# dt and B with all 128 rows in layer 1, and the side work's balance by place

## The chip, the cores and the metric

The kernel runs on one core of one Trainium2 chip. A core has five engines that work side by side and wait for one another through semaphores: TensorE (PE: multiplies and transposes, from SBUF into PSUM), VectorE (DVE), ScalarE (ACT), GpSimd (POOL) and SyncE (SP, which here issues transfers). PEld is TensorE's loading of weights. The metric is the device time of one execution in microseconds, and the number told is the median of several runs.

## The reference

Two layers work on an image of 256 x 256 positions with 128 channels, in fp32; each adds its result to the image. Layer 0 is triangle attention over rows. Layer 1, which the change touches, is a window scan:

```python
x = x + _L0_conv_ref(_gn(x), ...)          # triangle attention
x = x + _L1_conv_ref(_gn(x), ...)          # window scan
# in _L1_conv_ref
x_dbl = jnp.einsum('bkdl,kcd->bkcl', xs, x_proj_w)
dts, Bs, Cs = jnp.split(x_dbl, [DT_RANK, DT_RANK + D_STATE], axis=2)
dts = jnp.einsum('bkrl,kdr->bkdl', dts, dt_projs_w)
dts = jax.nn.softplus(dts + dt_projs_b[None, :, :, None])
def step(h, inp):
    u, dt, Bl, Cl = inp
    dA = jnp.exp(dt[..., None] * A)
    h = h * dA + (dt * u)[..., None] * Bl[:, :, None, :]
    y = jnp.einsum('bkdn,bkn->bkd', h, Cl)
    return (h, y)
```

Each image position is expanded to 256 inner channels, convolved 3 x 3 per channel, gated with silu, and cut into windows of 8 x 8. Two windows are merged into a sequence of 128 steps, which is walked in four ways (K = 4): two orders, each forward and backward. dt has rank 8 (DT_RANK), the state has 16 entries (D_STATE). After the scan come a layer norm, a gate from z, and a projection back to 128 channels.

## The kernel before, in words

**Bands, jobs, units.** Layer 1 is cut into 64 bands of 16 image rows by 64 columns. A band has two groups of four sequences, and each group is walked in two orders (`o`): so there are four jobs a band and 256 in all. A job is 32 units: two directions (`back`), four quarters of the state (`q`), two halves of the inner channels (`dh`), two halves of the sequences (`p`). A unit's number modulo 32 is its place in the job.

**A unit's work.** `decay` (L1172, ScalarE) makes exp(dt*A), four instructions for two units. `input` (L1185, TensorE) makes dt*u*B in PSUM, in the tile `b_p`, which has two buffers: it multiplies rows of `dut` (the transposed dt*u) with a diagonal arrangement of B, 64 rows at a time. `scan` (L1205, VectorE) runs the recurrence over 1024 columns. `weigh` (L1212, GpSimd) multiplies two units' states with C. `reduce` (L1223, TensorE) adds the weighed states into `y_p` by transposes, 16 for two units.

**The order.** The loop from L1333 writes each engine's order out by hand. At an even unit i it issues the decay of units i+4 and i+5, the input of unit i+1, the scan of unit i and the input of unit i+2. At an odd unit it issues the scan, the weigh of the pair, and the reduce of the pair two behind. `input` of unit i+2 needs the buffer that the scan of unit i frees.

**A job's preparation.** `own_script` (L1118) prepares the next job at fixed places: u at 7 and 9, `xd` (dt's 8 raw rows for each direction with a row of ones for the bias, then B, then C, 128 rows in all) at 15 to 17, B's transposes `bt_mm` at 18, their copy `bt_ev` at 19, and the forward dt at 20 to 26; `script` (L1091) does the backward dt at 0 to 6. Each dt is made in two halves: a matmul `dt_mm` into PSUM, softplus's Exp and Ln on ScalarE a unit later (`dt_act`), then one operation on VectorE (`dt_max`, L1034) at the places 2, 6, 22 and 26. `xd`, `bt`, `dt` and others share one PSUM buffer, named `side`. The copy `bt` is sent to DRAM by eight small transfers (`spread`, place 20), into zeroed blocks from which B's diagonal arrangement is read back. `xd`'s last 32 rows go to DRAM as C.

**The balance of side work.** What belongs to no job (the in projection, the convolution, the gate, the norm, the out projection) is a queue of small steps, `Filler`, each with a cost: columns of TensorE where positive, 0 for ScalarE's steps, -2 for VectorE's, which run at even units alone. At each unit the credit rises by `rate` columns up to `cap`; the job's own calls at this place are taken off it; and at odd units steps of TensorE are run while the credit is no less than their cost less `slack`. After a step of another engine, no step of TensorE follows in that unit.

Of the kernel before, what the change touches and what calls it, by code (L numbers as in the profile page):

```python
# [12 lines left out]
F32 = mybir.dt.float32  # L13
# [6 lines left out]
P = 128  # L20
# [5 lines left out]
DI = 256  # L26
NS = 16
DTR = 8
# [8 lines left out]
NBLK = 4  # L37
# [30 lines left out]
def kernel(  # L68
# [28 lines left out]
    nc = tc.nc  # L97
# [10 lines left out]
    ident = const.tile([P, P], F32, name="ident")  # L108
# [50 lines left out]
    wts = ctx.enter_context(tc.tile_pool(name="wts", bufs=1))  # L159
# [8 lines left out]
    for dh in range(2):  # L168
        nc.scalar.dma_start(
            out=wtap[:, dh], in_=conv_w[:, dh * P : (dh + 1) * P].rearrange("t d -> d t")  # L170
# [5 lines left out]
    for dh in range(2):  # L176
        for k in range(KD):
            o, back = k % 2, k // 2
            for at, lo, n in (
# [5 lines left out]
                    out=wx[:, dh, o, at : at + n],  # L185
                    in_=x_proj[dh * P : (dh + 1) * P, k, lo : lo + n],
                )

    wdt = wts.tile([P, 2, DI], F32, name="wdt")
    for back in range(2):  # L190
        at = 32 * back
        nc.scalar.dma_start(
            out=wdt[at : at + DTR], in_=dt_w[:, 2 * back : 2 * back + 2]
        )
        for o in range(2):
            for dh in range(2):
                j = 2 * (o + 2 * back) + dh
                nc.scalar.dma_start(
                    out=wdt[at + DTR : at + DTR + 1, o, dh * P : (dh + 1) * P],
                    in_=dt_b[:, j : j + 1].rearrange("p j -> j p"),  # L200
                )
    units_at = wts.tile([P, 1], F32, name="units_at")
# [13 lines left out]


    perm = wts.tile([P, 2, P], F32, name="perm")
    permt = wts.tile([P, 2, P], F32, name="permt")
    halves_of = ident.rearrange("p (y f x) -> p y f x", y=WIN, f=2)  # L220
    for o, positions in enumerate(hilbert_positions()):
        for s, (wy, wx_) in enumerate(positions):
# [1 line left out]
                perm[:, o, 2 * s : 2 * s + 2], halves_of[:, wy, :, wx_]  # L224
            )
    with tc.tile_pool(name="pmp", bufs=1, space=PSUM) as pp:
        pt_p = pp.tile([P, 2, P], F32, name="pt_p")
        for o in range(2):
            nc.tensor.transpose(pt_p[:, o], perm[:, o], ident)
        nc.vector.tensor_copy(permt, pt_p)  # L230

        ca_p = pp.tile([P, P], F32, name="ca_p")
        nc.tensor.matmul(ca_p, perm[:, 0], perm[:, 1], start=True, stop=True)
        carry = wts.tile([P, P], F32, name="carry")
        nc.vector.tensor_copy(carry, ca_p)
# [25 lines left out]
    with tc.tile_pool(name="lnc", bufs=1) as cp, tc.tile_pool(  # L261
        name="lnx", bufs=3
    ) as xp, tc.tile_pool(name="lnt", bufs=3) as tp, tc.tile_pool(
        name="lnp", bufs=2, space=PSUM
# [9 lines left out]
        for k in range(KD):  # L274
            for nh in range(2):
                for blk in range(NBLK):
                    nc.scalar.dma_start(
                        out=bdiag[k][nh][blk].rearrange("p t n -> p (t n)"), in_=zero
# [33 lines left out]
    with tc.tile_pool(name="atc", bufs=1) as cp, tc.tile_pool(  # L312
        name="atx", bufs=7
    ) as xp, tc.tile_pool(name="att", bufs=3) as tp, tc.tile_pool(
        name="ats", bufs=8
    ) as wp, tc.tile_pool(name="atps", bufs=1, space=PSUM) as ps_s, tc.tile_pool(
        name="atpt", bufs=1, space=PSUM
    ) as ps_t, tc.tile_pool(name="atpm", bufs=1, space=PSUM) as ps_m, tc.tile_pool(
        name="atpo", bufs=1, space=PSUM
# [11 lines left out]
        for mc in range(2):  # L331
            nc.sync.dma_start(
                out=trib[:, :, mc, :],
                in_=tri_d[:, mc * P : (mc + 1) * P, :].rearrange("h p n -> p h n"),
# [333 lines left out]
    class Band:  # L668
# [125 lines left out]
        def finish(self, g):  # L794

            if self.gated is None:
                self.gated = one_p.tile([P, 2, NSEQ, SEQ], F32, name="gated")
            for s2 in range(GS // 2):
                s = g * GS + 2 * s2
                yield 512  # L800
                z_p = fill("z_p")
                for dh in range(2):
                    nc.tensor.matmul(
                        z_p[:, dh * DI : (dh + 1) * DI],
                        win[:, DI + dh * P : DI + (dh + 1) * P],
                        self.xg[:, 1 : 1 + WIN, :, 1 + s * WIN : 1 + (s + 2) * WIN]
                        .rearrange("p y f x -> p (y f) x")
                        .rearrange("p y (s x) -> p s y x", s=2),
                        start=True,
                        stop=True,  # L810
                    )
                yield -2

                ysum = self.ysb[g, 1][:, 2 * s2 : 2 * s2 + 2]
                e = two_p.tile([P, 512], F32, name="e")
                nc.vector.tensor_scalar(e, z_p, FLOOR, None, ALU.max)
                st = two_p.tile([P, 2, 6], F32, name="st")
                mv = two_p.tile([P, 2, 2], F32, name="mv")
                for j in range(2):
                    nc.vector.bn_stats(st[:, j], ysum[:, j])  # L820
                for j in range(2):
                    nc.vector.bn_aggr(mv[:, j], st[:, j])
                yield 0
                logistic(e)
                rs = two_p.tile([P, 2], F32, name="rs")
                rsqrt(rs, mv[:, :, 1])
                neg = two_p.tile([P, 2], F32, name="neg")
                nc.scalar.activation(neg, rs, AF.Copy, scale=-1.0)
                nb = two_p.tile([P, 2], F32, name="nb")
                for j in range(2):  # L830
                    nc.scalar.activation(
                        nb[:, j : j + 1],
                        mv[:, j, 0:1],
                        AF.Identity,
                        scale=neg[:, j : j + 1],
                    )
                yield -2
                nc.vector.tensor_mul(e, e, z_p)
                yn = one_p.tile([P, 2, DI], F32, name="yn")
                for j in range(2):  # L840
                    nc.scalar.activation(
                        yn[:, j],
                        ysum[:, j],
                        AF.Identity,
                        bias=nb[:, j : j + 1],
                        scale=rs[:, j : j + 1],
                    )
                yield 256
                w_p = fill("w_p")
                for dh in range(2):  # L850
                    for j in range(2):
                        nc.tensor.transpose(
                            w_p[:, dh * DI + j * P : dh * DI + (j + 1) * P],
                            yn[:, j, dh * P : (dh + 1) * P],
                            permt[:, 1],
                        )
                yield 0
                for dh in range(2):
                    half = w_p[:, dh * DI : (dh + 1) * DI]
                    nc.scalar.activation(  # L860
                        half,
                        half,
                        AF.Identity,
                        bias=lb1[:, dh : dh + 1],
                        scale=lw1[:, dh : dh + 1],
                    )
                yield -2
                nc.vector.tensor_mul(
                    self.gated[:, :, s : s + 2].rearrange("p d s l -> p d (s l)"),
                    w_p.rearrange("p (d l) -> p d l", d=2),  # L870
                    e.rearrange("p (d l) -> p d l", d=2),
                )
# [26 lines left out]
    def token_blocks(t):  # L899

        return t.rearrange("c (h s t) -> c h s t", h=2, s=GS)
# [5 lines left out]
    class Job:  # L907
# [53 lines left out]
        def bt_mm(self):  # L961
            self.c_d = cdr.tile([2 * NS, GT], F32, name="c_d")
            for h in range(2):
                nc.sync.dma_start(
                    out=token_order(self.c_d)[:, h],
                    in_=token_blocks(self.xd[96:128])[:, h],
                )
            self.bt_p = side("bt_p")
            for i in range(NBLK):
                nc.tensor.transpose(  # L970
                    self.bt_p[:, i * 32 : (i + 1) * 32],
                    self.xd[64:96, i * P : (i + 1) * P],
                    ident[64:96, 64:96],
                )

        def bt_ev(self):
            self.bt = two_p.tile([P, NBLK, 2, NS], F32, name="bt")
            nc.scalar.copy(
                self.bt.rearrange("p b k n -> p (b k n)"), self.bt_p[:, 0 : NBLK * 32]
            )  # L980

        def spread(self):
# [31 lines left out]

        def dt_mm(self, back, dh):
            self.dt_p = side("dt_p")
            rows = slice(32 * back, 32 * back + DTR + 1)
            nc.tensor.matmul(  # L1018
                token_order(self.dt_p),
                wdt[rows, self.o, dh * P : (dh + 1) * P],  # L1020
                token_blocks(self.xd[rows]),
                start=True,
                stop=True,
            )
# [93 lines left out]
        def own_script(self):  # L1118
# [6 lines left out]
                15: [(512, lambda: self.xd_mm(0))],  # L1125
                16: [(512, lambda: self.xd_mm(1))],
                17: [(0, lambda: self.xd_ev())],
                18: [(128, lambda: self.bt_mm())],
                19: [(0, lambda: self.bt_ev())],
                20: [(512, lambda: self.dt_mm(0, 0)), (0, lambda: self.spread())],  # L1130
                21: [(0, lambda: self.dt_act(0, 0))],
# [159 lines left out]

    rate, cap, slack = 350, 800, 128
    with tc.manual_schedule():
        bands[0].load()
        run(bands[0].normalise(), bands[0].expand(), bands[0].conv(0))
# [5 lines left out]
        for c in range(2):  # L1303
            job, back, q = quads[c]
# [28 lines left out]
        for i, unit in enumerate(units):  # L1333
# [15 lines left out]
            if i % 2:  # L1349
# [4 lines left out]
                if i >= 5:  # L1354
                    units[i - 5].reduce()
                    units[i - 4].reduce()
            credit = min(credit + rate, cap)
            for cost, call in calls:
                credit -= cost
                call()  # L1360
# [81 lines left out]
```

## Time and profile before

| What | Value |
|---|---|
| Median of 3 runs | 23599.31 us (23597.42 to 23599.98) |
| Profiled execution | 23598.3 us, its span 23596.4 us |
| Granted TensorE clock, mean | 0.997 |
| PE busy | 22824.2 us, 97% |
| DVE busy | 21652.4 us, 92% |
| ACT busy | 18542.0 us, 79% |
| POOL busy | 21292.1 us, 90% |

The profile is of one execution. A row of a group shows the line and engine, the operation and its tiles (written <- read), its shape and count, then its busy time and mean length in ns, and after the bar how long the engine idled just before it and for whom. A row of the timeline shows start and length in us; neighbours of the same line are merged. The ends of TensorE's instructions are modelled, their starts are recorded.

### The profile page before, as it was taken

To read this page: it belongs to the slowest core of one execution; us is meant where nothing else is said; L and a number is where in the kernel's file an instruction comes from. 1 tells how busy PE (TensorE), PEld (TensorE's weight loads), DVE (VectorE), ACT (ScalarE), POOL (GpSimd) and SP (SyncE) were. 2 spreads that over 40 slices of the span, in tenths; PEclk is the share of its full clock that TensorE was granted. 3 is DMA by queue.
4 is the path that set the end of the run, shared out by engine and by line. 5 is a ranking of instruction groups with operands and counts; after the bars stand their busy time and mean duration, and the time that the engine had idled before them with its cause. 6 is when DMAs were issued, how large, how long until landed. Compare 5 with 4: busy or idle time off the path is not lost.

```text
span 23596.4 us, 427303 instructions
## 1 busy us (share of the span) xinstructions
PE 22824.2 (97%) x171020; PEld 16986.3 (72%) x171020; DVE 21652.4 (92%) x17940; ACT 18542.0 (79%) x35206; POOL 21292.1 (90%) x5966
## 2 busy tenths in 40 slices
PE   7999999999999999999999999999999999999999
PEld 2555677777777777777777777777777777777777
DVE  6888899999999999999999999999999999999998
ACT  5999777777777777777777777777777777777777
POOL 3777899999999999999999999999999999999999
PEclk9999999999999999999999999999999999999999
DMA  5222444444444444444444444444444444444444
GB/s 200 76 74 72 146 160 159 161 162 160 161 158 162 161 160 159 160 163 160 161 159 160 162 160 162 158 161 162 160 159 161 162 161 160 158 161 162 160 160 147
DMA packets 2000327, 3638.76 MB, mean 154 GB/s; under 512 B 1129584, under 2 KB 1131760, under 8 KB 1725824
## 3 DMA queue, kind: packets, MB, share of 16 engines
q1 hardware_dynamic: 1985616, 3602.35, 45.7%
q8 instruction: 1347, 22.07, 0.4%
q10 hardware_dynamic: 12720, 9.07, 0.1%
q14 instruction: 644, 5.28, 0.1%
HBM read 3467.33 MB, written 143.65 MB: 153 GB/s over the span
## 4 chain that ended last, share of the span: by engine, by line
PE 67%; DVE 16%; ACT 9%; issue 8%; DMA 0%; ACTq 0%; POOLq 0%; SPq 0%; POOL 0%; DVEq 0%
PE b_p L1185 23%; PE y_p L1223 21%; DVE h L1205 14%; PE dt_p L1018 4%; PE cv_p L769 4%; PE xd_p L949 2%; ACT da L1172 2%; PE aT_p L522 1%; PE dut_p L1052 1%; PE sc L465 1%; ACT w_p L860 1%; PE in_p L721 1%; PE o_p L885 1%; ACT e L132 1%; PE v_p L383 1%
## 5 line engine op out<-in xcount | busy, mean ns | idle before, releaser
L1212 POOL TENSOR_TENSOR h<-h,cc 128x2048 f32<-128x2048 f32 x4096 | 18598.0, 4551 | 1318.2 <-POOL h L1212 560.7
L1205 DVE TENSOR_TENSOR_SCAN h<-da,b_p 128x1024 f32<-128x1024 f32 x8192 | 18245.8, 2271 | 1212.6 <-PE b_p L1185 1193.2
L1172 ACT ACTIVATE da<-dt,am 128x508 f32<-128x508 f32 x16384 | 10396.5, 707 | 853.3 <-DVE h L1205 853.2
L1185 PE MATMUL b_p<-diag,dut 64*128 64x256 f32 x65536 | 8561.4, 395 | 430.0 <-DVE h L1205 365.7
L1223 PEld LDWEIGHTS y_p<-ident,h 128*128 128x128 f32 x65536 | 7130.2, 140 | 1408.4 <-issue 1296.3
L1223 PE MATMUL y_p<-ident,h 128*128 128x128 f32 x65536 | 8008.8, 276 | 25.1 <-issue 19.4
L1185 PEld LDWEIGHTS b_p<-diag,dut 64*128 64x128 f32 x65536 | 5851.7, 186 | 2916.9 <-issue 1331.2
L738 ACT ACTIVATE tap<-xin,wtap 128x512 f32<-128x512 f32 x2048 | 1504.2, 744 | 349.1 <-PE cv_p L769 349.0
L1041 POOL TENSOR_TENSOR du<-dt,u 128x512 f32<-128x512 f32 x1024 | 1309.1, 1278 | 57.9 <-DVE dt L1034 57.9
L769 PE MATMUL cv_p<-ident,tap 128*128 128x128 f32 x9216 | 1273.7, 275 | 5.1 <-DVE xct L788 3.8
L769 PEld LDWEIGHTS cv_p<-ident,tap 128*128 128x128 f32 x9216 | 1047.4, 141 | 232.4 <-issue 228.2
L1028 ACT ACTIVATE sp<-dt_p 128x512 f32<-128x512 f32 x1024 | 603.1, 589 | 777.5 <-PE dt_p L1018 777.5
L452 POOL TENSOR_TENSOR tm<-trib,mb 128x2048 f32<-128x2048 f32 x256 | 1167.1, 4559 | 10.7
L1018 PE MATMUL dt_p<-xd,wdt 9*128 9x512 f32 x2048 | 1149.8, 641 | 2.5 <-DVE dt L1034 2.2
L493 ACT ACTIVATE at<-at,nmax 128x256 f32<-128x256 f32 x2048 | 1019.5, 502 | 0.0
L1061 ACT COPY dut<-dut_p 128x512 f32<-128x512 f32 x1024 | 583.8, 570 | 292.9 <-PE dut_p L1052 292.9
L1163 ACT ACTIVATE da<-ident 128x16 f32<-128x16 f32 x1536 | 346.0, 225 | 549.2 <-DVE h L1205 547.4
L1029 ACT ACTIVATE sp<-sp,one 128x512 f32<-128x512 f32 x1024 | 743.1, 726 | 33.3
L729 ACT COPY xin<-in_p 128x440 f32<-128x440 f32 x384 | 201.7, 525 | 718.6 <-PE in_p L721 718.6
L478 DVE CUSTOM_DVE_ANT_0 at<-sc,tm 128x256 f32<-128x256 f32 x2048 | 738.1, 417 | 7.9 <-PE sc L465 7.4
L1034 DVE SCALAR_TENSOR_TENSOR dt<-sp,dt_p 128x512 f32<-128x512 f32 x1024 | 677.9, 662 | 13.9 <-ACT sp L1029 13.9
L1052 PE MATMUL dut_p<-ident,du 128*128 128x128 f32 x4096 | 650.2, 281 | 13.7 <-ACT dut L1061 8.7
(132 smaller groups left out, 15502.6 us busy)
## 6 DMA issues: line engine op xcount, KB each, us to landing
cc<-c_d SPq DMA_DIRECT2D x2048, 1024.0 KB
diag<-z SPq DMA_DIRECT2D x1024, 1024.0 KB
xt<-in_x_dram SPq DMA_DIRECT2D x16, 2048.0 KB
xt<-in_x_dram SPq DMA_DIRECT2D x32, 1024.0 KB
xn_d<-xn SPq DMA_DIRECT2D x32, 1024.0 KB
xn<-xn_d SPq DMA_DIRECT2D x128, 256.0 KB
mb<-in_mask_dram SPq DMA_DIRECT2D x128, 256.0 KB
xr<-in_x_dram SPq DMA_DIRECT2D x128, 256.0 KB
```

What stands on the lines that cost most here:

```text
L452: nc.gpsimd.tensor_add(self.tm, trib.rearrange("p h m n -> p (h m) n"), self.pair.mb[:, self.row].unsqueeze(1).to_broadcast([P, 2 * NH, IMG]),
L493: nc.scalar.activation(self.at[hp][:, j, :], self.at[hp][:, j, :], AF.Exp, bias=self.nmax[hp][:, j : j + 1], scale=-1.0, accum_out=self.de ...
L738: nc.scalar.activation(scaled.rearrange("p s (y x) -> p s y x", x=WIN), self.xin[:, dh] .rearrange("p y f x -> p (y f) x")[:, 2 * dy : 2 * ...
L769: nc.tensor.matmul(cv_p[:, s], now[:, s], ident, start=(tap == 0 and s == 0), stop=(tap == 8 and s == GS - 1), is_transpose=True, skip_gro ...
L1018: nc.tensor.matmul(token_order(self.dt_p), wdt[rows, self.o, dh * P : (dh + 1) * P], token_blocks(self.xd[rows]), start=True, stop=True,)
L1041: nc.gpsimd.tensor_mul(token_blocks(du), token_order(self.dt[back][dh]), token_blocks(self.u[:, dh]),)
L1052: nc.tensor.transpose(self.dut_p[:, h * DI + dh * P : h * DI + (dh + 1) * P], self.du[back][dh][:, (2 * h + p) * P : (2 * h + p + 1) * P], ...
L1172: nc.scalar.activation(da[:, :, j, lo:hi], dt[:, :, lo:hi], AF.Exp, scale=am[:, a0 : a0 + 1])
L1185: nc.tensor.matmul(b_p[:, s, :, h * 64 : (h + 1) * 64].rearrange("p n t -> p t n"), job.dut[self.back][rows, p, h, self.dh * P : (self.dh ...
L1205: nc.vector.tensor_tensor_scan(out=out_, data0=d0, data1=d1, initial=0.0, op0=ALU.mult, op1=ALU.add)
L1212: nc.gpsimd.tensor_mul(self.pair, self.pair, cc.rearrange("p n s t -> p s n t"))
L1223: nc.tensor.matmul(job.y_p[:, 2 * p + s, self.dh * P : (self.dh + 1) * P], self.h[:, s, j], ident, start=(first and s == 0 and j == 0), st ...
```

## The change

Three things change.

`wdt`, dt's weights, gets 128 rows for each direction, zeroed first, with the direction's nine rows filled in; `dt_mm` multiplies all 128 rows of `xd` with them in place of nine. `bt_mm` transposes all 128 rows of `xd` in four blocks of 128 columns in place of its 32 rows of B, so the PSUM tile is filled whole; `bt_ev` copies the 32 columns of B out of each block. `bt` has one buffer in place of two, and its cost in the balance is 256 columns in place of 128. `permt` loses a half that nothing reads.

The balance's `rate` falls from 350 to 320 columns a unit, and at the places 1, 5, 21 and 25 a unit gets 200 more: 32 x 350 = 11200 columns a job before, 32 x 320 + 4 x 200 = 11040 after.

```diff
--- before.py
+++ after.py
@@ -186,17 +186,19 @@
                     in_=x_proj[dh * P : (dh + 1) * P, k, lo : lo + n],
                 )
 
-    wdt = wts.tile([P, 2, DI], F32, name="wdt")
+
+    wdt = wts.tile([P, 2, 2, DI], F32, name="wdt")
+    nc.vector.memset(wdt, 0.0)
     for back in range(2):
         at = 32 * back
         nc.scalar.dma_start(
-            out=wdt[at : at + DTR], in_=dt_w[:, 2 * back : 2 * back + 2]
+            out=wdt[at : at + DTR, back], in_=dt_w[:, 2 * back : 2 * back + 2]
         )
         for o in range(2):
             for dh in range(2):
                 j = 2 * (o + 2 * back) + dh
                 nc.scalar.dma_start(
-                    out=wdt[at + DTR : at + DTR + 1, o, dh * P : (dh + 1) * P],
+                    out=wdt[at + DTR : at + DTR + 1, back, o, dh * P : (dh + 1) * P],
                     in_=dt_b[:, j : j + 1].rearrange("p j -> j p"),
                 )
     units_at = wts.tile([P, 1], F32, name="units_at")
@@ -216,7 +218,7 @@
 
 
     perm = wts.tile([P, 2, P], F32, name="perm")
-    permt = wts.tile([P, 2, P], F32, name="permt")
+    permt = wts.tile([P, P], F32, name="permt")
     halves_of = ident.rearrange("p (y f x) -> p y f x", y=WIN, f=2)
     for o, positions in enumerate(hilbert_positions()):
         for s, (wy, wx_) in enumerate(positions):
@@ -224,9 +226,8 @@
                 perm[:, o, 2 * s : 2 * s + 2], halves_of[:, wy, :, wx_]
             )
     with tc.tile_pool(name="pmp", bufs=1, space=PSUM) as pp:
-        pt_p = pp.tile([P, 2, P], F32, name="pt_p")
-        for o in range(2):
-            nc.tensor.transpose(pt_p[:, o], perm[:, o], ident)
+        pt_p = pp.tile([P, P], F32, name="pt_p")
+        nc.tensor.transpose(pt_p, perm[:, 1], ident)
         nc.vector.tensor_copy(permt, pt_p)
 
         ca_p = pp.tile([P, P], F32, name="ca_p")
@@ -852,7 +853,7 @@
                         nc.tensor.transpose(
                             w_p[:, dh * DI + j * P : dh * DI + (j + 1) * P],
                             yn[:, j, dh * P : (dh + 1) * P],
-                            permt[:, 1],
+                            permt,
                         )
                 yield 0
                 for dh in range(2):
@@ -968,15 +969,16 @@
             self.bt_p = side("bt_p")
             for i in range(NBLK):
                 nc.tensor.transpose(
-                    self.bt_p[:, i * 32 : (i + 1) * 32],
-                    self.xd[64:96, i * P : (i + 1) * P],
-                    ident[64:96, 64:96],
+                    self.bt_p[:, i * P : (i + 1) * P],
+                    self.xd[:, i * P : (i + 1) * P],
+                    ident,
                 )
 
         def bt_ev(self):
-            self.bt = two_p.tile([P, NBLK, 2, NS], F32, name="bt")
+            self.bt = two_p.tile([P, NBLK, 2, NS], F32, name="bt", bufs=1)
             nc.scalar.copy(
-                self.bt.rearrange("p b k n -> p (b k n)"), self.bt_p[:, 0 : NBLK * 32]
+                self.bt.rearrange("p b k n -> p b (k n)"),
+                self.bt_p.rearrange("p (b r) -> p b r", b=NBLK)[:, :, 64:96],
             )
 
         def spread(self):
@@ -1014,11 +1016,10 @@
 
         def dt_mm(self, back, dh):
             self.dt_p = side("dt_p")
-            rows = slice(32 * back, 32 * back + DTR + 1)
             nc.tensor.matmul(
                 token_order(self.dt_p),
-                wdt[rows, self.o, dh * P : (dh + 1) * P],
-                token_blocks(self.xd[rows]),
+                wdt[:, back, self.o, dh * P : (dh + 1) * P],
+                token_blocks(self.xd),
                 start=True,
                 stop=True,
             )
@@ -1125,7 +1126,7 @@
                 15: [(512, lambda: self.xd_mm(0))],
                 16: [(512, lambda: self.xd_mm(1))],
                 17: [(0, lambda: self.xd_ev())],
-                18: [(128, lambda: self.bt_mm())],
+                18: [(256, lambda: self.bt_mm())],
                 19: [(0, lambda: self.bt_ev())],
                 20: [(512, lambda: self.dt_mm(0, 0)), (0, lambda: self.spread())],
                 21: [(0, lambda: self.dt_act(0, 0))],
@@ -1291,7 +1292,8 @@
 
 
 
-    rate, cap, slack = 350, 800, 128
+
+    rate, more, cap, slack = 320, 200, 800, 128
     with tc.manual_schedule():
         bands[0].load()
         run(bands[0].normalise(), bands[0].expand(), bands[0].conv(0))
@@ -1354,7 +1356,7 @@
                 if i >= 5:
                     units[i - 5].reduce()
                     units[i - 4].reduce()
-            credit = min(credit + rate, cap)
+            credit = min(credit + rate + more * (place in (1, 5, 21, 25)), cap)
             for cost, call in calls:
                 credit -= cost
                 call()
```

## The prediction

> **What bounds the kernel.** I read the page first, for its chain and its costliest groups. The scans of layer 1 run from 2439.3 us to 23553.7 us (first and last start of the scan line): 21114.4 us for 64 bands, 329.9 us a band of 128 units, so this loop is 89% of the span and the change lies in it. These rows say who sets its pace:
>
> ```profile
> PE 67%; DVE 16%; ACT 9%; issue 8%; DMA 0%; ACTq 0%; POOLq 0%; SPq 0%; POOL 0%; DVEq 0%
> ...
> L1205 DVE TENSOR_TENSOR_SCAN h<-da,b_p 128x1024 f32<-128x1024 f32 x8192 | 18245.8, 2271 | 1212.6 <-PE b_p L1185 1193.2
> ```
>
> TensorE holds two thirds of the chain, and VectorE's scan idles 1193 us for TensorE's b_p: 18.6 us a band. GpSimd isn't on the chain. So TensorE time pays, but only in pairs of units where the scan really waits. The timeline of one stretch shows which. First VectorE's scans, two to a row, in brackets the wait before the odd unit's scan:
>
> ```profile
> 9999.49 4.46 DVE L1205 TENSOR_TENSOR_SCAN h<-da,b_p 128x1024 f32<-128x1024 f32 x2 [1.14 <-PE b_p L1185]
> 10004.54 4.46 DVE L1205 TENSOR_TENSOR_SCAN h<-da,b_p 128x1024 f32<-128x1024 f32 x2 [0.58 <-PE b_p L1185]
> 10009.85 4.46 DVE L1205 TENSOR_TENSOR_SCAN h<-da,b_p 128x1024 f32<-128x1024 f32 x2 [0.27 <-PE b_p L1185]
> 10015.31 4.46 DVE L1205 TENSOR_TENSOR_SCAN h<-da,b_p 128x1024 f32<-128x1024 f32 x2 [0.99 <-PE b_p L1185]
> ```
>
> Odd scan to odd scan: 5.05, 5.31, 5.46 us. Then TensorE in the same stretch, start and length of each block:
>
> ```profile
> 9989.94 1.97 PE L1223 MATMUL y_p<-ident,h 128*128 128x128 f32 x16
> 9991.75 1.02 PE L949 MATMUL xd_p<-u,wx 128*128 128x512 f32 x2
> 9992.70 2.00 PE L1185 MATMUL b_p<-diag,dut 64*128 64x256 f32 x16
> 9994.63 1.12 PE L949 MATMUL xd_p<-u,wx 128*128 128x512 f32 x2
> 9995.59 1.91 PE L1223 MATMUL y_p<-ident,h 128*128 128x128 f32 x16
> 9997.34 1.04 PE L769 MATMUL cv_p<-ident,tap 128*128 128x128 f32 x8
> ...
> 10000.23 0.43 PE L970 MATMUL bt_p<-ident,xd 32*128 32x32 f32 x4
> 10000.60 1.97 PE L1223 MATMUL y_p<-ident,h 128*128 128x128 f32 x16
> ...
> 10005.28 1.12 PE L1018 MATMUL dt_p<-xd,wdt 9*128 9x512 f32 x2
> 10006.33 1.97 PE L1223 MATMUL y_p<-ident,h 128*128 128x128 f32 x16
> 10008.14 0.60 PE L769 MATMUL cv_p<-ident,tap 128*128 128x128 f32 x4
> 10008.67 2.00 PE L1185 MATMUL b_p<-diag,dut 64*128 64x256 f32 x16
> 10010.59 1.97 PE L1223 MATMUL y_p<-ident,h 128*128 128x128 f32 x16
> 10012.49 1.12 PE L1018 MATMUL dt_p<-xd,wdt 9*128 9x512 f32 x2
> 10013.54 0.65 PE L769 MATMUL cv_p<-ident,tap 128*128 128x128 f32 x4
> ```
>
> Ends are modelled, so only differences of starts count. A block costs more wherever the height of the rows in use changes (64 in b_p, 128 in y_p, 9 or 32 in dt_p and bt_p).
>
> **Part 1, dt with 128 rows.** At an even place dt stands between b_p and y_p: 10006.33-10005.28 = 1.05, and y_p after it takes 1.81. The full-height neighbour of the same size, xd_p, takes 0.96 there (9994.63 to 9995.59) and leaves y_p at 1.75: saving 0.09+0.055 = 0.145 us. At an odd place dt stands behind y_p: y_p takes 1.90 (10010.59 to 10012.49) in place of 1.81, dt 1.05, and the transposes behind it 0.58 in place of 0.53. At full height two such multiplies between full-height blocks cost 0.86 (0.95 of xd_p at 9991.75, less the 0.09 of the step to b_p). So dt's share is 1.05+0.09+0.055 = 1.20 before a transpose and 1.05 before b_p, against 0.86: saving 0.34 or 0.19. The weights are zero in the added rows; columns stay 512.
>
> Two rules of the Trainium skill differ here. "TensorE: Matmul & The Clock Gate", section LDWEIGHTS, has time go by columns, not rows, and its Part 3 lets small-row matmuls run beside others: by these dt gains nothing or loses an overlap. "TensorEngine Tiling (Array Packing)", Key Properties: changing the tiling mode drains TensorE. The trace sides with the second: dt's columns equal xd's, yet a block more is lost on each side, and nothing overlaps dt (b_p's own halves do start in twos). By the first rule the sum below would be +0.2 us a band, by the rows it is -2.0.
>
> **Part 2, bt with 128 rows.** Now 10000.60-10000.23 = 0.37 with y_p 1.80 behind. Four full transposes cost like dut_p at the same kind of place (in the same view 10026.02 to 10026.52, 0.50, y_p then 1.75): +0.08 us, once a job. Its copy takes the same 128 columns (250 ns row), in steps through PSUM now; that form has no row, so 0.16 (its spacing unstalled) to 0.58 us (all 512 columns, the skip row's spacing). I take 0.16: ScalarE waits for other engines around place 19 either way, and at 0.58 only dt's first multiply, a unit later, could feel it. With one bt buffer the copy waits for the previous job's spread of it, issued a job (some 82 us) earlier: nothing, unless that landing were 80 us late.
>
> **Start.** One memset of 1024 columns (wx's 512 took 0.48, so 1 us), one transpose fewer. The wdt loads issue at 29 us, behind wx's, and VectorE waits for x meanwhile: nothing; uncovered 1 us.
>
> **Part 3, the balance.** I followed the credit by its own lines, unit by unit, for a band; it repeats each band under both settings, and both end a band with the same work done. Call pair m units 2m and 2m+1 of the band. The period of a pair is the larger of two:
> VectorE: 4.38 (two scans of 2.19) plus its side operations at the NEXT even place (0.56 for dt's and most; 1.44 for z's with statistics).
> TensorE: 3.82 (b_p 1.93 + y_p 1.80 + 0.09) plus the pair's extras: 0.44 for each four transposes, 0.74 in_p, 0.86 carry, o_p, odd xd (0.91 even), 0.99 z_p, and dt and bt as above. Where the odd scan waited under 0.44 us, TensorE starts its loop at the even scan's end, and 0.44 less that delay is added (0.12 to start, 0.10 to refill, 1.18 from b_p's first multiply to the scan, less the 0.97 of b_p's first half).
> So a pair ahead of dt's VectorE operation hides 0.56 us of TensorE work. Check on the rows: bt 0.36+carry gives 5.04 (5.05 seen); dt 1.05+transposes 0.44 gives 5.31 (5.31); dt 1.20+0.44 gives 5.46 (5.46). Over all 64 pairs this, with the gated product's wait for ScalarE (1.27 us after b_p starts), gives 329.8 against 329.9.
>
> Now the changed plan, by stretches of pairs, worked before -> after:
> Pairs 0-3: 20.62 -> 20.24. A convolution step leaves pair 1 (5.46 to 4.68, dt 0.86 and no transposes), joins pair 2 (4.94 to 5.27).
> Pairs 9-14: 32.02 -> 31.37. z_p leaves pair 9 for 10, w_p 11 for 12; pair 9 falls 1.44, pair 10 rises 1.08 as z's statistics now add to dt's operation at place 22.
> Pairs 16-17: 9.74 -> 10.27. An o_p arrives.
> Pairs 24-30: 35.01 -> 34.76. in_p goes from 24 to 26.
> Pairs 32-36: 26.54 -> 26.52. Three steps in pair 32.
> Pairs 38-45: 40.80 -> 40.04. Pair 43 5.46 to 4.68.
> Pairs 57-63: 36.08 -> 35.61. Pair 58 to 4.94 (now VectorE's 4.38+0.56), 59 to 4.90, 60 and 61 to 5.13 (three transposes blocks 1.31+3.82).
> Sum -0.38-0.65+0.53-0.25-0.02-0.76-0.47 = -2.00 us a band; 64 bands -128 us. The forms alone under the old plan come to -2.35, the plan alone with the old forms to -0.1: the new plan keeps most of the gain, and adds none to it. No wait is added; GpSimd, next in line, needs 16x4.55+4x1.28 = 78 us (rows of h and du) a job of 82.5.
>
> The profiled execution took 23598.3 us (span 23596.4), the median of the runs is 23599.3: 23470 against the first, **23471 us** against the median.
>
> **Rivals.**
> (a) Height brings nothing: dt's extra comes from its output in steps of 64 columns, which xd lacks. For: the forms do differ in that. Against: the loss sits in the neighbours' starts. Then +0.08 a job and the plan: +0.2 a band, **23610**, no change.
> (b) Slower: 119 more rows lower the granted clock. The page grants 9 tenths or more in every slice (mean 0.997). Place: the 67% of the chain that is TensorE's. Price: 1% of clock 0.67x21114/100 = 141 us. It decides from 1.2% (128+47 us): at 1.5% **23680**. Against: zero weights, and all but dt, bt and b_p is full height already.
> (c) ScalarE late: at places 22 to 25 z's logistic (2.9 us) and dt's Exp and Ln (1.26) now follow one another before yn, on which w_p waits. Worked out, yn is ready 0.5 us ahead of w_p. 1 us later costs 0.5 us a band: 23500, inside the range.
>
> **How the numbers follow.** The worked case, (c) in it, 0.85, its own range 23420 to 23522 (0.8 us a band either way); (a) 0.09; (b) 0.06. 0.2% is 47 us, about what a measurement tells from no change. Faster 0.85, same 0.09, slower 0.06. The range 23405 to 23535 holds the worked case nearly whole and reaches part of the way to (a).
>
> **What would show it.** dt_p to y_p 0.96 and y_p to dt_p 1.80 in the timeline; bt_p to y_p 0.50; the scan's wait for b_p down from 1193 by some 90 us or more; a band of 327.9 us; pairs 9 and 43 shorter, 10 and 16 longer by the amounts above. It is wrong if dt keeps its 1.05, or if new waits (VectorE for ScalarE, w_p for yn) take over 1 us a band.

## The result, and the profile after

The changed kernel takes **23482.76 us** (median of 6 runs, 23479.83 to 23484.05); the kernel before, on the same chip, 23598.83 us (6 runs, 23597.42 to 23599.98). The ratio is 0.9951, with a 95% interval of 0.9938 to 0.9964: 116 us faster. The forecast was 23471 us with a range of 23405 to 23535; it was 12 us too low.

The span of the profiled execution is 23479.8 us at a mean granted clock of 0.997, as before. The two rows that answer to those of before, the chain by engine and the scan's group:

```profile
PE 65%; DVE 18%; issue 8%; ACT 8%; DMA 0%; ACTq 0%; POOL 0%; POOLq 0%; DVEq 0%; SPq 0%
...
L1206 DVE TENSOR_TENSOR_SCAN h<-da,b_p 128x1024 f32<-128x1024 f32 x8192 | 18233.2, 2270 | 1107.8 <-PE b_p L1186 1069.5
```

Two points of the chain have gone from TensorE to VectorE, and the scan waits 1069.5 us for b_p where it waited 1193.2: 124 us less; all its idle time fell by 105 us (1212.6 to 1107.8), and the span by 117. These sums move with the gain and are not the gain itself. The scans now run from 2439.3 to 23436.5 us, 328.08 us a band where it was 329.91. Outside the loop nothing moved: 1.83 x 64 = 117 us is all of it.

The timeline of TensorE in the stretch that the prediction showed (the same places of a band):

```profile
9956.89 0.66 PE L971 MATMUL bt_p<-ident,xd 128*128 128x128 f32 x4
9957.38 1.91 PE L1224 MATMUL y_p<-ident,h 128*128 128x128 f32 x16
9959.13 1.02 PE L1070 MATMUL y_p<-ysb,carry 128*128 128x512 f32 x2
...
9962.01 1.13 PE L1019 MATMUL dt_p<-xd,wdt 128*128 128x512 f32 x2
9962.97 1.91 PE L1224 MATMUL y_p<-ident,h 128*128 128x128 f32 x16
9964.81 2.11 PE L1186 MATMUL b_p<-diag,dut 64*128 64x256 f32 x16
9966.85 1.97 PE L1224 MATMUL y_p<-ident,h 128*128 128x128 f32 x16
9968.65 1.02 PE L1019 MATMUL dt_p<-xd,wdt 128*128 128x512 f32 x2
9969.51 0.60 PE L770 MATMUL cv_p<-ident,tap 128*128 128x128 f32 x4
9970.04 2.00 PE L1186 MATMUL b_p<-diag,dut 64*128 64x256 f32 x16
```

Start to start, dt at an even place takes 0.96 us (9962.01 to 9962.97; 1.05 before). At an odd place y_p takes 1.80 ahead of it (9966.85 to 9968.65; 1.90 before), dt 0.86 (1.05), and the transposes behind it 0.53 (0.58). bt takes 0.49 and y_p behind it 1.75; behind dt at 9962.97 it takes 1.84, since b_p follows and the 0.09 of that step is in it. One more number in this fence matters below: the b_p that starts at 9964.81 takes 2.04 us, where b_p otherwise takes 1.93.

VectorE's scans in that stretch, pairs 57 to 59, two to a row, the odd unit's first:

```profile
9956.14 4.46 DVE L1206 TENSOR_TENSOR_SCAN h<-da,b_p 128x1024 f32<-128x1024 f32 x2 [1.14 <-PE b_p L1186]
9961.26 4.46 DVE L1206 TENSOR_TENSOR_SCAN h<-da,b_p 128x1024 f32<-128x1024 f32 x2 [0.66 <-PE b_p L1186]
9965.65 0.66 DVE L1035 SCALAR_TENSOR_TENSOR dt<-sp,dt_p 128x512 f32<-128x512 f32 x1
9966.23 4.46 DVE L1206 TENSOR_TENSOR_SCAN h<-da,b_p 128x1024 f32<-128x1024 f32 x2
9971.22 4.46 DVE L1206 TENSOR_TENSOR_SCAN h<-da,b_p 128x1024 f32<-128x1024 f32 x2 [0.54 <-PE b_p L1186]
```

Odd scan to odd scan it is now 5.12, 4.97 and 4.99 us, where the prediction's stretch had 5.05, 5.31 and 5.46. In the middle pair no wait is left in the row: the scan follows dt's VectorE operation directly.

The stretch of the band where the steps of z (the gate) have moved, again on VectorE, before and then after:

```profile
9752.66 4.45 DVE L1205 TENSOR_TENSOR_SCAN h<-da,b_p 128x1024 f32<-128x1024 f32 x2
9757.03 0.66 DVE L816 TENSOR_SCALAR e<-z_p 128x512 f32<-128x512 f32 x1
9757.62 0.74 DVE L820 BATCH_NORM_STATS2 st<-ysb 128x6 f32<-128x256 f32 x2
9758.27 0.30 DVE L822 BATCH_NORM_AGGREGATE mv<-st 128x2 f32<-128x6 f32 x2
9758.49 4.43 DVE L1205 TENSOR_TENSOR_SCAN h<-da,b_p 128x1024 f32<-128x1024 f32 x2
9762.84 0.67 DVE L1034 SCALAR_TENSOR_TENSOR dt<-sp,dt_p 128x512 f32<-128x512 f32 x1
9763.42 0.68 DVE L838 TENSOR_TENSOR e<-e,z_p 128x512 f32<-128x512 f32 x1
9764.01 4.46 DVE L1205 TENSOR_TENSOR_SCAN h<-da,b_p 128x1024 f32<-128x1024 f32 x2
...
9710.20 8.81 DVE L1206 TENSOR_TENSOR_SCAN h<-da,b_p 128x1024 f32<-128x1024 f32 x4
9718.92 0.66 DVE L1035 SCALAR_TENSOR_TENSOR dt<-sp,dt_p 128x512 f32<-128x512 f32 x1
9719.67 0.69 DVE L817 TENSOR_SCALAR e<-z_p 128x512 f32<-128x512 f32 x1
9720.28 0.74 DVE L821 BATCH_NORM_STATS2 st<-ysb 128x6 f32<-128x256 f32 x2
9720.94 0.30 DVE L823 BATCH_NORM_AGGREGATE mv<-st 128x2 f32<-128x6 f32 x2
9721.16 4.43 DVE L1206 TENSOR_TENSOR_SCAN h<-da,b_p 128x1024 f32<-128x1024 f32 x2
9725.50 0.66 DVE L839 TENSOR_TENSOR e<-e,z_p 128x512 f32<-128x512 f32 x1
9726.08 4.46 DVE L1206 TENSOR_TENSOR_SCAN h<-da,b_p 128x1024 f32<-128x1024 f32 x2
```

After the change four scans run without a break (pair 9, 4.37 us where it was 5.83), and z's operation and the statistics stand behind dt's, in pair 10: 6.58 us where it was 5.52. Of the two pairs together 0.40 us is left as a gain.

### The profile page after: what moved, and what is told of

The parts are those of the page before. It is cut to its first block, busy times and chain, and to the rows that moved or that the text cites. A ratio compares the mean times of both kernels' runs of the same rounds, so it can differ in the third digit from the quotient of the medians.

```text
span 23479.8 us, 427750 instructions
## 1 busy us (share of the span) xinstructions
PE 22636.8 (96%) x171019; PEld 17043.0 (73%) x171019; DVE 21673.9 (92%) x17941; ACT 18543.1 (79%) x35206; POOL 21292.5 (91%) x5966
## 3 DMA queue, kind: packets, MB, share of 16 engines
q14 instruction: 648, 5.31, 0.1%
## 4 chain that ended last, share of the span: by engine, by line
PE 65%; DVE 18%; issue 8%; ACT 8%; DMA 0%; ACTq 0%; POOL 0%; POOLq 0%; DVEq 0%; SPq 0%
PE b_p L1186 22%; PE y_p L1224 21%; DVE h L1206 15%; PE dt_p L1019 4%; PE cv_p L770 4%; PE xd_p L950 2%; ACT da L1173 2%; PE dut_p L1053 1%; PE aT_p L523 1%; PE sc L466 1%; ACT w_p L861 1%; PE in_p L722 1%; DVE gated L869 1%; PE o_p L886 1%; DVE dt L1035 1%
## 5 line engine op out<-in xcount | busy, mean ns | idle before, releaser
L1206 DVE TENSOR_TENSOR_SCAN h<-da,b_p 128x1024 f32<-128x1024 f32 x8192 | 18233.2, 2270 | 1107.8 <-PE b_p L1186 1069.5
L770 PE MATMUL cv_p<-ident,tap 128*128 128x128 f32 x9216 | 1218.2, 273 | 5.1 <-DVE xct L789 3.8
L1019 PE MATMUL dt_p<-xd,wdt 128*128 128x512 f32 x2048 | 1100.6, 619 | 2.5 <-DVE dt L1035 2.2
```

The lines of the kernel that those rows point to most:

```text
L770: nc.tensor.matmul(cv_p[:, s], now[:, s], ident, start=(tap == 0 and s == 0), stop=(tap == 8 and s == GS - 1), is_transpose=True, skip_gro ...
L1019: nc.tensor.matmul(token_order(self.dt_p), wdt[:, back, self.o, dh * P : (dh + 1) * P], token_blocks(self.xd), start=True, stop=True,)
L1206: nc.vector.tensor_tensor_scan(out=out_, data0=d0, data1=d1, initial=0.0, op0=ALU.mult, op1=ALU.add)
```

## The experiments

The prediction said that dt's form saves the time because the height of the rows changes at dt's edges, that bt's form costs a little, and that the balance adds nothing. Rivals on record were that height brings nothing, that the clock falls, and that the added rows act by their number rather than by the change of height. Each experiment undoes or isolates one of these. Every time is a median of four runs (of ten for the balance alone and for bt alone), beside the kernel before on the same chip (23600.72 or 23600.45 us). Behind it stand the lowest and highest run, then the ratio to the kernel before with its 95% interval.

**The forms without the new balance.** The changed kernel with the old settings:

```diff
-    rate, more, cap, slack = 320, 200, 800, 128
+    rate, more, cap, slack = 350, 0, 800, 128
```

> The changed kernel with the old balance (350 columns at every place; bt still counted as 256). Theory: the gain is TensorE's, from no change of row height around dt; the new balance only spends some of it. Then the pair periods sum to 2.35 us a band less than before: 23449 us (0.9936 of before), some 34 us faster than the changed kernel. Rival: the balance (more columns ahead of dt's VectorE operation) makes the gain; then most of the 116 us goes and this stays near 23590.

Measured: 23459.16 us (23458.38 to 23460.94), 0.9940 [0.9925, 0.9955]; a band takes 327.71 us. So the forms alone are worth 142 us, some 25 us more than with the change's own balance (116). The intervals of the two kernels overlap, the spreads of their runs do not, and their bands differ by 0.37 us. bt's count of 256 is still in this kernel.

**The balance without the forms.** The kernel before with

```diff
-                18: [(128, lambda: self.bt_mm())],
+                18: [(256, lambda: self.bt_mm())],
...
-    rate, cap, slack = 350, 800, 128
+    rate, more, cap, slack = 320, 200, 800, 128
...
-            credit = min(credit + rate, cap)
+            credit = min(credit + rate + more * (place in (1, 5, 21, 25)), cap)
```

> The old forms of dt (9 rows) and bt (32 rows) with the new balance (320, and 200 more at places 1, 5, 21, 25; bt counted as 256). Theory: the sum of pair periods falls by only 0.06 us a band: 23595 us, no measurable change. Rival (the balance makes the gain): about 23490.

Measured: 23600.75 us (23598.01 to 23604.41), 1.0000 [0.9991, 1.0009]; a band takes 329.93 us. Nothing, as worked. The scan's row of VectorE's waits, columns total, number and longest:

```profile
DVE h L1205 <- PE b_p L1185: 1173.7, 1855, 1.8
```

The total wait is 20 us shorter than before with no time gained. Single pairs change their length, in both directions (pair 9 from 5.83 to 4.37 us, pair 10 from 5.52 to 6.73), and the sum stays. A shorter wait is a gain only when the pairs are shorter in sum.

**dt's form alone.** The kernel before with dt at 128 rows, bt and the balance as they were (`bt` with one buffer and `permt` halved, for the room that `wdt` needs):

```diff
-    wdt = wts.tile([P, 2, DI], F32, name="wdt")
+    wdt = wts.tile([P, 2, 2, DI], F32, name="wdt")
+    nc.vector.memset(wdt, 0.0)
...
-                wdt[rows, self.o, dh * P : (dh + 1) * P],
-                token_blocks(self.xd[rows]),
+                wdt[:, back, self.o, dh * P : (dh + 1) * P],
+                token_blocks(self.xd),
```

> Before, with only dt at 128 rows; bt_p from 32 rows, old balance, bt counted as 128. Theory: 2.38 us a band less, 23447 us; dt_p to y_p 0.96 us, dt_p between full-height blocks 0.86. Rival (bt's form matters as much as dt's): only about half of that, 23520.

Measured: 23454.90 us (23453.37 to 23456.05), 0.9938 [0.9921, 0.9954]; a band takes 327.66 us. All of the gain is dt's: 146 us.

**dt with 64 rows.** The same with 64 rows in place of 128, which tells the number of rows from the change of height:

```diff
-                wdt[:, back, self.o, dh * P : (dh + 1) * P],
-                token_blocks(self.xd),
+                wdt[0:64, back, self.o, dh * P : (dh + 1) * P],
+                token_blocks(self.xd[0:64]),
```

> As the kernel with dt alone, but dt multiplies 64 rows (the height of b_p) in place of 128. Theory (it is the change of height that costs): at even places, and at odd ones before b_p, one step falls away as with 128 rows; at odd places before a transpose (6 of 8 a band) two steps stay, about 1.2 us as with 9 rows. The pair periods give 1.48 us a band less than before: 23504 us. Rival (few rows make a multiply slow, not the change): 64 rows are full enough, dt costs 0.86 everywhere as with 128: 23447 us. Rival (only 128 rows are quick): 23599.

Measured: 23500.42 us (23498.42 to 23502.87), 0.9957 [0.9943, 0.9972]; a band takes 328.39 us. TensorE's timeline in this kernel:

```profile
9968.70 2.00 PE L1184 MATMUL b_p<-diag,dut 64*128 64x256 f32 x16
9970.53 1.02 PE L1017 MATMUL dt_p<-xd,wdt 64*128 64x512 f32 x2
9971.48 1.97 PE L1222 MATMUL y_p<-ident,h 128*128 128x128 f32 x16
9973.28 0.60 PE L769 MATMUL cv_p<-ident,tap 128*128 128x128 f32 x4
...
9975.74 1.96 PE L1222 MATMUL y_p<-ident,h 128*128 128x128 f32 x16
9977.63 1.12 PE L1017 MATMUL dt_p<-xd,wdt 64*128 64x512 f32 x2
9978.68 0.66 PE L769 MATMUL cv_p<-ident,tap 128*128 128x128 f32 x4
9979.27 2.00 PE L1184 MATMUL b_p<-diag,dut 64*128 64x256 f32 x16
```

At an even place, behind b_p's 64 rows, no change of height is left on dt's near side: b_p takes 1.83 (9968.70 to 9970.53) in place of 1.93 and dt 0.95 in place of 1.05, but the change to 128 now lies between dt and y_p, and y_p keeps its 1.80. At an odd place, between blocks of 128 rows, dt costs just what it did with nine: y_p ahead 1.89, dt 1.05, the transposes 0.59. So seven times the rows gain nothing there. What costs is the change, once on each side. (At even places 64 rows are thus the better form by 0.055 us; 64 at even and 128 at odd places together was not tried.)

**bt's form alone.** The kernel before with bt at 128 rows, counted 128 as before:

```diff
-                    self.bt_p[:, i * 32 : (i + 1) * 32],
-                    self.xd[64:96, i * P : (i + 1) * P],
-                    ident[64:96, 64:96],
+                    self.bt_p[:, i * P : (i + 1) * P],
+                    self.xd[:, i * P : (i + 1) * P],
+                    ident,
```

> Before with only bt at 128 rows, counted as 128 columns, old balance. Theory: 0.08 us more of TensorE once a job, 0.31 us a band: 23619 us, hardly told from no change. Rival (leaving the 32-row height pays here as with dt): faster than before by up to 30 us.

Measured: 23618.41 us (23616.2 to 23622.85), 1.0008 [0.9998, 1.0018]; a band takes 330.22 us, 0.31 more. That is the 0.08 us a job of the prediction, four times. The interval just holds 1; the two spreads of runs don't meet. bt's transposes have four times the columns, and that outweighs the one change of height that they save (from 64 rows to 32 and on to 128 there were two, now there is one, from 64 to 128). In the forms together bt's share is smaller, 23459 against 23455 with dt alone; there its count of 256 moves side steps too, which was not taken apart.

**Another balance on the changed kernel.** The rule of pairs in the prediction was followed over other settings, and two were taken: one near the old rate, and the one whose sum came out smallest.

```diff
-    rate, more, cap, slack = 320, 200, 800, 128
+    rate, more, cap, slack = 340, 0, 800, 128
```

> The changed kernel with 340 columns at every place and none added anywhere. The theory of pair periods, followed through the balance as before: the changed kernel's places are no optimum; at an even 340 the gate's w_p no longer waits for yn and the steps fall into better pairs: 325.7 us a band against 327.8, so 256 us under before: 23344 us. Rival (columns ahead of dt's VectorE operation are what makes the balance good): slower than the changed kernel's 23483 and than the old balance's 23459.

Measured: 23412.46 us (23407.54 to 23415.64), 0.9921 [0.9906, 0.9935]; a band takes 326.89 us.

```diff
-    rate, more, cap, slack = 320, 200, 800, 128
+    rate, more, cap, slack = 325, 0, 900, 64
```

> The changed kernel with 325 columns at every place, cap 900 and slack 64. Theory: 325.2 us a band, 289 us under before: 23311 us, the fastest of all. Rival: a lower rate starves the side work and bunches it at the band's end: slower than 23483.

Measured: 23382.69 us (23381.90 to 23385.47), 0.9908 [0.9894, 0.9923]; a band takes 326.53 us. It is the fastest kernel of this study, 100 us faster than the change and 218 us faster than the kernel before. Its scan's row of waits:

```profile
DVE h L1206 <- PE b_p L1186: 967.7, 2036, 7.2
```

The scan waits 102 us less than in the changed kernel (1069.5).

**That balance on the kernel before.** One line:

```diff
-    rate, cap, slack = 350, 800, 128
+    rate, cap, slack = 325, 900, 64
```

> Before with 325 columns at every place, cap 900, slack 64, and the old forms of dt and bt. Theory: the balance alone can bring as much as the forms if its steps fall well: 2.0 us a band less than before, 23474 us. Rival (only TensorE's forms matter, the balance moves waits about): 23600.

Measured: 23509.56 us (23499.80 to 23513.89), 0.9961 [0.9947, 0.9976]; a band takes 328.46 us. So 91 us were to be had by the balance alone with the old forms, by rate, cap and slack together (they were not tried one by one), and not by the places that the change chose. The gains add up roughly: dt's form is worth 146 us, this balance 91, both (with bt's form, which costs) 218.

All three settings fell short of what was worked for them: by 68 us, 72 us and 36 us. A part of it is TensorE's clock. Its timeline in the fastest kernel, first a long band and then the same place of the next band:

```profile
9696.81 1.13 PE L1186 MATMUL b_p<-diag,dut 64*128 64x256 f32 x8 [0.74 <-DVE h L1206]
9698.99 2.08 PE L1186 MATMUL b_p<-diag,dut 64*128 64x256 f32 x8 [1.04 <-DVE h L1206]
9701.00 1.11 PE L1053 MATMUL dut_p<-ident,du 128*128 128x128 f32 x4
9701.91 2.17 PE L1224 MATMUL y_p<-ident,h 128*128 128x128 f32 x16
9703.92 0.60 PE L853 MATMUL w_p<-permt,yn 128*128 128x128 f32 x4
...
10024.87 1.13 PE L1186 MATMUL b_p<-diag,dut 64*128 64x256 f32 x8 [0.74 <-DVE h L1206]
10027.05 1.13 PE L1186 MATMUL b_p<-diag,dut 64*128 64x256 f32 x8 [1.04 <-DVE h L1206]
10028.11 0.66 PE L1053 MATMUL dut_p<-ident,du 128*128 128x128 f32 x4
10028.61 1.91 PE L1224 MATMUL y_p<-ident,h 128*128 128x128 f32 x16
10030.35 0.60 PE L853 MATMUL w_p<-permt,yn 128*128 128x128 f32 x4
```

From the second half of b_p to w_p it is 4.93 us in the one and 3.30 in the other, with the same instructions behind the same waits. The granted clock tells the two apart. Here are two neighbouring stretches of 3.41 us of the long band, then two of the next band. A row has the stretch and its length, busy us and instructions of PE, PEld, DVE, ACT and POOL, then the granted clock, the DMA share and GB/s:

```profile
9695.61:9699.02 3.41, 1.63 (x15) 0.94 (x12) 3.41 (x3) 3.31 (x11) 2.93 (x2) 1.00 0.00 0
9699.02:9702.44 3.42, 3.42 (x15) 2.60 (x16) 3.42 (x3) 1.76 (x4) 3.02 (x2) 0.50 0.03 7
...
10023.29:10026.71 3.42, 1.98 (x16) 1.29 (x14) 3.42 (x2) 3.32 (x10) 2.95 (x2) 1.00 0.00 0
10026.71:10030.12 3.41, 3.07 (x26) 2.69 (x27) 3.41 (x4) 2.43 (x5) 3.02 (x2) 1.00 0.02 5
```

In the long band both waits for the scan fall into one stretch, TensorE is busy for 1.63 of its 3.41 us, and in the next stretch it is granted half the clock (0.50). In the other band it is busy for 1.98 of 3.42 us and keeps the clock. 14 of the 64 bands are longer in this way: 14 x 1.63 = 23 us of the 72. The setting with rate 340 has 14 such bands too (23 us of 68), and 325 with the old forms has three bands with two such stretches each, 3.3 us a band (10 us of 36). The kernel before and the changed kernel have none in the loop.

## Why the prediction was right

**Part 1** held to a hundredth: 0.96 at the even place, with 1.75 for y_p where transposes follow (pair 42), and 0.86 between full-height blocks at the odd one. dt alone gave 146 us, and 64 rows showed that it is the change of height and not the number of rows. Of the two rules that the prediction weighed, that of the Trainium skill's page "TensorEngine Tiling (Array Packing)", Key Properties, by which a change of the tiling mode drains TensorE, fits: dt with 64 rows is cheap beside b_p's 64 and dear between 128s. Time by columns alone, the other rule, would have made all three heights equal; they differ by 146 us and by 46 us (64 rows against 128). **Rival (a)** falls with the same runs.

**Part 2** held: 0.31 us a band measured alone, 0.08 x 4 = 0.32 worked. bt's copy added nothing beyond it (median 247 ns, before 248), in the changed kernel ScalarE never waits for a transfer ahead of that copy, as a late single buffer would show, and **the start** nothing: the first scan starts at 2439.3 us in both kernels.

**Part 3** held in its signs and nearly in its sizes. The forms under the old balance were worked at -2.35 us a band and gave -2.20; the change at -2.00 and gave -1.83; the balance with the old forms at -0.1 and gave nothing. So the new balance gives back 0.37 us a band of what the forms save (worked 0.35). The forms under the old rate keep bt's count of 256, and outside pairs 24 to 44 their pairs are as long as the changed kernel's: the moves of z and of pairs 1 and 2 come with that count, and the new rate with its four places acts in pairs 24 to 44 alone, at a loss.

The pairs, as medians over the bands, odd scan to odd scan in us (the worked lengths of pairs 36, 41 and 62 are of the same working, which prints only some pairs):

| Pair | Before | After | Worked after |
|---|---|---|---|
| 1 | 5.46 | 4.68 | 4.68 |
| 2 | 4.96 | 5.29 | 5.27 |
| 43 | 5.46 | 4.68 | 4.68 |
| 36 | 4.70 | 5.28 | 5.16 |
| 41 | 5.06 | 5.24 | 5.13 |
| 59 | 5.46 | 5.00 | 4.90 |
| 62 | 5.07 | 5.13 | 5.02 |

**The term that was mis-sized** is TensorE's refill after a stall, 0.10 us of the 0.44 in the prediction's rule. Where the stall works out at nothing or nearly so, the 0.10 was left out; the trace has it there too. In the b_p from 9964.81 the second half starts on time, 0.97 us after the first, but its next multiplies come 0.32 us later, as at the start of a block, and not 0.22: b_p takes 2.04 us and not 1.93. Pairs 36, 41 and 59 have this refill after the change and are 0.10 to 0.12 us longer than worked. Pairs 3 and 61 had it before and have it no more; in pair 3 it was left out of the working before too (5.01, worked 4.91). Pair 62 is another case: its b_p has no refill; VectorE's product behind the two scans starts 4.52 us into the pair, before 4.46, and why was not followed.

By the prediction's stretches of pairs (means over the bands, worked in brackets): -0.49 (-0.38), -0.62 (-0.65), +0.50 (+0.53), -0.23 (-0.25), +0.09 (-0.02), -0.65 (-0.76), -0.43 (-0.47), in sum -1.83 (-2.00). The first is the refill that pair 3 lost, the fifth and sixth are those of pairs 36 and 41. The 0.17 us a band left are 11 of the 12 us between forecast and result. That it is no more is in part luck: the term was missing before the change too, and a part of it cancelled.

The other balances have more such pairs. Those in which b_p's second half comes less than 0.12 us late and is refilled all the same number 7 a band before, 10 in the changed kernel, 13 at rate 340, 14 at 325 and 11 at 325 with the old forms. At 0.10 us the 6, 7 and 4 added ones would be 38, 45 and 26 us; with the half clock's 23, 23 and 10 us that is 61, 68 and 36 us of the 68, 72 and 36 that were missing. This is an estimate from a count, and no run isolated the refill. The count does not fit everywhere: by it the change would have missed 19 us and not 12, and the balance without the forms, with two such pairs fewer than before, gained nothing.

**Rival (b)** is out: the clock is 0.997 before and after, with 119 rows more. **Case (c)** did not come: before, the gated product at the end of pair 11 waited 0.69 us for w_p; now, at the end of pair 12, it stands behind dt's operation and waits for nothing. VectorE's wait for w_p at this line fell from 161.4 to 118.8 us in all, and it does so with the balance alone too (119.7) and with the old rate once bt counts 256 (118.5).

## What to carry to other kernels

Among full-height matmuls, fill a small one's rows up with zeros when its columns stay the same (dt: 146 us of 23600), but not when that multiplies its columns (bt: 18 us lost). When side work is spread by a credit, work out each pair of the loop with what bounds it, and count a stall as dear however short it is; here that found a setting worth 91 us alone, beside 116 for the change. Then read the granted clock stretch by stretch: a mean of 0.996 in place of 0.997 hid 14 stretches of half clock. A change of two things needs each run alone: here one half brought the gain, and the other gave some of it back.

## What the runs showed of the hardware that was not expected

A change of row height on TensorE costs by the edge: about 0.09 us where a block of 128 rows is left, about as much where 64-row b_p goes over to a block of another height (1.83 us when it need not, 1.93 when it must), and the rest in the block behind. One edge fewer saves 0.145 us at the even place, two fewer 0.34 us at the odd one. Nine rows or 64 made no difference between blocks of 128.

TensorE's granted clock can halve for a moment inside a loop that keeps it 97% busy. In every trace here the stretches of half clock last 3.41 us or a multiple of it (the last one is cut by the end), and they start on one grid of 3.413 us. In the two changed kernels with rates 340 and 325, every stretch of this grid in the loop (2500 to 23300 us) in which TensorE was busy for 49.1% or less was followed by one of half clock, 28 in all, and none in which it was busy for 49.3% or more. Before the change the least busy stretch there has 60.8%, after it 59.3%, and neither is followed by half clock. Busy time is not the whole rule: with the old forms at 325 the half clock followed three stretches of 49.6 to 50.3%, none of the next ones from 50.6% on, and yet three of 72.9%; in the balance without the forms it followed one of 72.1%.

The grid also tells which bands are hit. A band of 326.43 us is 95.6 of its steps, so the same two waits fall differently in each band; four bands with one long one are 1307.3 us, 383 steps, and in the fastest kernel mostly every fourth band is long. This is read from the traces; no run changed these waits alone, and where the second kind of half clock (after 72%) comes from stays open.
